# A transformer block's second norm, transposed by VectorE in 32x32 blocks instead of by TensorE

## The chip, the cores and the metric

One core of a Trainium2 chip runs the whole program. Its engines are TensorE (PE; its weight loads are listed apart as PEld), VectorE (DVE), ScalarE (ACT), GpSimd (POOL) and SyncE (SP), which mostly issues DMAs. The metric is the time on the device in microseconds (us) of one execution. The kernel before took 651.25 us, the median of three runs (650.94 to 652.86).

## The reference

Sixteen batches of 256 tokens with 256 features pass through one block in float32: a norm, attention with 16 heads of 16 features, a residual; a second norm, a gated feed-forward network with 1024 inner features, a residual. Cut to what matters:

```python
x = x + attn(layernorm(x), wq, wk, wv, wo)      # scores masked beyond 16 keys ahead, softmax
h = layernorm(x)                                # the second norm
gate = einsum('bsh,ih->bsi', h, gate_w)         # gate_w, up_w, down_w: Catmull-Rom
up   = einsum('bsh,ih->bsi', h, up_w)           # splines through control points
x = x + einsum('bsi,hi->bsh', silu(gate) * up, down_w)
```

The product of h with the gate and up weights sums over the features. On the chip that sum runs over partitions, so h, which the norm leaves with tokens on the partitions, has to be turned so that features lie there.

## The kernel before, in words

All of it is one software pipeline. The loop at the end of `block_kernel` runs 20 steps `s`; step `s` works on four batches at once: it projects queries, keys and values of batch `s+3`, takes row maxima of the scores of batch `nb = s-1`, exponentials and value products of batch `tb = s-2`, and the output projection, second norm and feed-forward network of `ob = s-3` and of the batch before it. Each engine runs its instructions in the order in which the source writes them: the class `InOrder` (line 78; its call on line 88 is the line that nearly every record of the profile carries) hands each to a call that keeps program order. So what stands ahead of what on an engine is read off the source, and the text of the loop is the schedule.

A step has numbered gaps. `inner` (twice two groups of heads) and `outer` (twice) make the scores on TensorE; between them `project(s, gap)` and `fill(s, gap)` put other TensorE work. `fill` holds a table: for `s < 13` the products `gate_up` 1, 2 and 3 of batch `s-4` stand in gaps 1, 3 and 4, `down` 0 (the first 128 tokens) in gap 5 and `down` 1 in gap 6. From `s = 13` on, where nothing is left to project, `down` is cut into halves over gaps 4, 5, 6 and 6.5. `gate_up` 0 of batch `s-3` stands in gap 7, at the step's end.

The scores go to two PSUM tiles of which there is one copy each; ScalarE reads them with an exponential, VectorE with `find_max` (a reduction of 144 or 256 columns to a maximum per row, eight of them after the last `outer`). Both have to be through before TensorE writes the next scores there.

The part that the change touches is the tail of a step: `project_o` (attention output added to x), `stats_f` (mean and variance on VectorE, the power -1/2 on POOL), `fill(s, 5)`, `norm_f` (two VectorE instructions that write the normed batch, tile `xnf`, tokens on the partitions), the last `outer`, `fill(s, 6)`, `turn_f`, `project(s, 6)` (values projection, tile `pv`), `fill(s, 6.5)`, `turn_max` (the maxima transposed, tile `pm`) and `fill(s, 7)`. `turn_f` calls `transposed` (line 244): four TensorE passes of 128x128 against an identity into a PSUM tile `ptf`, then one ScalarE copy into `x2T`, which all the gate and up products of the batch read (`pg`, `pu`).

The tiles of `down` (`pd`) and of the gate and up products share two PSUM buffers, tag "f"; `ptf`, `pv`, `pm` and the projections share two others, tag "m". VectorE adds each finished `pd` to x.

Of the kernel before, what the change touches and what calls it, by code (L numbers as in the profile page):

```python
# [11 lines left out]
F32 = mybir.dt.float32  # L12
# [6 lines left out]
P = 128  # L19
B, S, DIM = 16, 256, 256  # L20
# [73 lines left out]
def block_kernel(  # L94
# [14 lines left out]
    pe, dve, act, pool, sp = (  # L109
        InOrder(tc, e) for e in (nc.tensor, nc.vector, nc.scalar, nc.gpsimd, nc.sync)  # L110
    )

    const = ctx.enter_context(tc.tile_pool(name="const", bufs=1))
    sb = ctx.enter_context(tc.tile_pool(name="sb", bufs=2))
# [100 lines left out]
    xns, mxs, aus, aos, recs, x2s, x2Ts = ({} for _ in range(7))  # L215
# [28 lines left out]
    def transposed(src, dst, nm, engine=act):  # L244

        pt = ps_m.tile([P, 2, S], F32, tag="m", name=f"p{nm}")
        for kc in range(2):
            for c in range(2):
                pe.transpose(
                    pt[:, kc, c * P : (c + 1) * P],  # L250
                    src[:, c, kc * P : (kc + 1) * P],
                    ident,
                )
        copied(engine, dst, pt)
# [110 lines left out]
    def scores(qk, maxima, g, first, to, n):  # L365

        half = slice(first % P, first % P + HB)
        for r in range(4):
            q4 = slice(32 * r, 32 * r + HD + (0 if maxima else 1))
            on = 0 if maxima else 1  # L370
            pe.matmul(
                tiles[r // 2][half, r % 2, to : to + n],
                lhsT=qk[q4, on, g, first : first + HB],
                rhs=qk[q4, 1 - on, g, 0:n] if maxima else qk[q4, 0, g, S - n : S],
                start=True,
                stop=True,
            )

    def find_max(b, g, r, c, at, n):
        h = 4 * g + r  # L380
        seen = sb.tile([P, S], BF16, tag="seen", name=f"z{b}_{h}_{c}")
        dve.tensor_tensor_reduce(
            out=seen[:, 0:n],
            in0=tiles[r // 2][:, r % 2, at : at + n],
            in1=masks[c],
            scale=1.0,
            scalar=NEG,
            op0=ALU.add,
            op1=ALU.max,
            accum_out=mxs[b][:, c, h : h + 1],  # L390
        )

    def read(exponentials, maxima):

        for stage, pr in ((exponentials, 0), (maxima, 1), (exponentials, 1), (maxima, 0)):
            if stage:
                stage(pr)
# [31 lines left out]
    def outer(nb, tb, g2):  # L429
        has_n, has_t = 0 <= nb < B, 0 <= tb < B  # L430
        qn, qt = qks[nb % NQK], qks[tb % NQK]
        for gi in range(2):
            g, at = 2 * g2 + gi, W0 * gi
            if has_n:
                scores(qn, True, g, 0, at, HB + LOOK)
                scores(qn, True, g, HB, at, P + LOOK)
            if has_t:
                scores(qt, False, g, P, at + HB + LOOK, W1)
                scores(qt, False, g, P + HB, at + JB, W1 - HB)
        def exponentials(pr):  # L440
            e = sb4.tile([P, 2, 2, W1], F32, tag="e1", name=f"e1{tb}_{g2}_{pr}")
            act.activation(
                e,
                tiles[pr][:, :, 0 : 2 * W0].rearrange("p r (g c) -> p r g c", g=2)[
                    :, :, :, W0 - W1 : W0
                ],
                AF.Exp,
                scale=HD**-0.5,
            )
            pool.affine_select(  # L450
                out=e[:, :, :, 0:P], in_=e[:, :, :, 0:P],
                compare_op=ALU.is_ge, fill=0.0, base=I1 + LOOK - P,
                pattern=[[0, 2], [0, 2], [1, P]], channel_multiplier=-1,
            )
            es[tb, 1, g2, pr] = e

        def maxima(pr):
            for r in (2 * pr, 2 * pr + 1):
                for gi in range(2):
                    find_max(nb, 2 * g2 + gi, r, 0, W0 * gi, JB)  # L460

        read(exponentials if has_t else None, maxima if has_n else None)
# [86 lines left out]
    def norm_f(b):  # L549
        x2s[b] = normed(b, "f")  # L550

    def turn_f(b):
        x2Ts[b] = sb.tile([P, 2, S], F32, tag="x2T", name=f"x2T{b}")
        transposed(x2s.pop(b), x2Ts[b], f"tf{b}")

    def product(out, lhsT, rhs, start, stop, columns=P):
# [29 lines left out]
    def down(b, c, half=None, columns=P):  # L586

        inter = inters[b]
        if (b, c) == (B - 1, 1):

            for n in range(0, DIM, P):
                at = slice(n, n + P)
                pd = ps_f.tile([P, P], F32, tag="f", name=f"pd{b}_{c}_{n}")
                for ic in range(8):
                    pe.matmul(
                        pd, lhsT=inter[:, ic, P:], rhs=downT[:, ic, at],
                        start=(ic == 0), stop=(ic == 7),
                    )
                dve.tensor_tensor(xs[b][:, c, at], xs[b][:, c, at], pd, ALU.add)
                (act if n else sp).dma_start(out[b][P:, at], xs[b][:, c, at])  # L600
            return
        if half != 1:
            pds[b, c] = ps_f.tile([P, DIM], F32, tag="f", name=f"pd{b}_{c}")
        for ic in range(8) if half is None else range(4 * half, 4 * half + 4):
            product(
                pds[b, c], inter[:, ic, c * P : (c + 1) * P], downT[:, ic, :], ic == 0, ic == 7,
                columns,
            )
        if half == 0:
            return  # L610
        dve.tensor_tensor(xs[b][:, c, :], xs[b][:, c, :], pds.pop((b, c)), ALU.add)
        to = out[b].rearrange("(c p) d -> p c d", p=P)
        if b == B - 1:
            sp.dma_start(to[:, c, :], xs[b][:, c, :])
        elif c == 1:
            sp.dma_start(to, xs.pop(b))
# [37 lines left out]
    def do(stage, b, *args):  # L654
        if 0 <= b < B:
            stage(b, *args)
# [8 lines left out]
    def fill(s, gap):  # L665


        if s < B - AHEAD:
            order = (
                (1, gate_up, 1, 32), (3, gate_up, 2), (4, gate_up, 3, 32), (5, down, 0),  # L670
                (6, down, 1),
            )
        else:
            order = (
                (1, gate_up, 1, 32), (2, gate_up, 2), (3, gate_up, 3), (4, down, 0, 0, 32),
                (5, down, 0, 1), (6, down, 1, 0), (6.5, down, 1, 1),
            )
        for at, stage, *what in order:
            if at == gap:
                if s == B + 3 and stage is down:  # L680

                    if what[1] == 0:
                        down(B - 1, what[0])
                else:
                    do(stage, s - 4, *what)
        if gap == 7:
            do(gate_up, s - 3, 0)
# [3 lines left out]
    def part(i):  # L691
        spline(*parts[i])

    early = {
        (0, 1): ((stats_a, 1), (value_ones, 1)),
        (0, 2): (
            (norm_a, 1), (project_qk, 0), (spread, 0), (load_rest, 0), (coefficients, 0),
            (stats_a, 2), (scores_and_values, 2),
        ),
        (0, 4): ((turn_a, 1, dve), (project_v, 0, dve), (norm_a, 2), (part, 0)),  # L700
        (1, 1): ((turn_a, 2), (project_part, 1, 0), (stats_a, 3)),
        (1, 2): ((project_part, 1, 1), (spread, 1), (coefficients, 1)),
# [50 lines left out]
    for s in range(B + 4):  # L753
        nb, tb, ob = s - 1, s - 2, s - 3
        inner(nb, tb, 0)
        if ob < B - 1:
            do(values, ob, 1)
            do(gather, ob)
        project(s, 1)
        fill(s, 1)  # L760
        inner(nb, tb, 1)
        do(invert, ob)
        if s:
            do(load_x, s + 2 + AHEAD)
        project(s, 2)
        fill(s, 2)
        outer(nb, tb, 0)
        project(s, 3)
        fill(s, 3)
        inner(nb, tb, 2)  # L770
        do(values, tb, 0)
        project(s, 4)
        do(divide, ob)
        fill(s, 4)
        inner(nb, tb, 3)
        do(project_o, ob)
        do(stats_f, ob)
        project(s, 5)
        fill(s, 5)
        if s != 3:  # L780
            do(norm_f, ob)
        outer(nb, tb, 1)
        fill(s, 6)
        if s == 3:

            project(s, 6)
            norm_f(ob)
            turn_max(nb)
        do(turn_f, ob)
        if s != 3:  # L790
            project(s, 6)
        fill(s, 6.5)
        if tb == B - 1:
            values(tb, 1)
            gather(tb)
        if s != 3:
            do(turn_max, nb)
        project(s, 7)
        fill(s, 7)
# [30 lines left out]
```

## Time and profile before

| what | value |
|---|---|
| median of 3 runs | 651.25 us |
| the profiled execution's own time | 652.13 us |
| its span, first to last instruction | 650.4 us |
| mean granted TensorE clock in it | 0.997 |
| TensorE / VectorE / ScalarE / POOL busy | 642.7 / 369.2 / 216.4 / 129.5 us |
| ptf: 64 TensorE passes, mean of one | 275 ns |
| x2T: 16 ScalarE copies, mean of one | 585 ns |
| gate product to gate product, batches 5 to 6 | 38.09 us |
| gate product to gate product, batches 10 to 11 | 32.91 us |

The profile is one execution, recorded instruction by instruction. A group line gives the count of its instructions, their busy time in us, the mean of one in ns, and behind the second bar the idle time of the engine ahead of them with what ended it. A timeline line gives start and duration in us, and the idle time ahead in brackets. A name such as `x2T<-ptf` says which tile is written from which. TensorE's records overlap, since its matmuls are pipelined, so the distance from the start of one group to the start of the next is what it costs there, not the duration.

### The profile page before, as it was taken

Reading aid. Unit: us, or ns where it says so; the run is one execution under the profiler, and the core shown is the slowest. Engines: PE = TensorE matmul, PEld = TensorE weight load, DVE = VectorE, ACT = ScalarE, POOL = GpSimd, SP = SyncE. Lnnn points to the kernel's source line nnn. Section 1 sums busy time; section 2 is a strip of 40 time slices with the busy share of each in tenths; the row PEclk is TensorE's granted clock in tenths of the full one; section 3 lists DMA queues with packets and bytes.
Section 4 is the critical chain, followed back from the end, with each engine's and each line's share of the span. In section 5 each row is a group of like instructions: output and inputs, shape, how many; then the busy total and the mean of one; then the engine's idle time right before and its main releaser. Section 6 shows DMA issues by size and latency. Waiting matters only on the chain.

```text
span 650.4 us, 21144 instructions
## 1 busy us (share of the span) xinstructions
PE 642.7 (99%) x8740; PEld 477.3 (73%) x8740; DVE 369.2 (57%) x1483; ACT 216.4 (33%) x383; POOL 129.5 (20%) x254
## 2 busy tenths in 40 slices
PE   8999999999999999999999999999999999999998
PEld 7666667777778777787877778777777777777777
DVE  6785566646465664646566464655656565633342
ACT  1345543233332323333232332323333333333110
POOL 6232222111121211212112121211212030312000
PEclk9999899999999999999999999999999999999999
DMA  5843141414132131312213131210010101010100
GB/s 173 174 69 54 35 83 29 82 38 86 34 76 42 35 75 39 86 35 69 49 31 80 36 72 34 54 32 21 19 36 20 36 21 30 26 41 14 51 17 17
DMA packets 40768, 33.36 MB, mean 51 GB/s; under 512 B 10593, under 2 KB 40033, under 8 KB 40673
## 3 DMA queue, kind: packets, MB, share of 16 engines
q1 hardware_dynamic: 39392, 30.90, 21.7%
q8 instruction: 69, 1.13, 0.8%
q10 hardware_dynamic: 1280, 1.11, 0.6%
q14 instruction: 27, 0.21, 0.3%
HBM read 14.42 MB, written 4.47 MB: 29 GB/s over the span
## 4 chain that ended last, share of the span: by engine, by line
PE 96%; DMA 1%; DVE 1%; ACT 1%; issue 1%; POOL 0%; SPq 0%; ACTq 0%
PE pg L88 18%; PE pd L88 17%; PE pu L88 17%; PE scores L88 15%; PE po L88 7%; PE py L88 5%; PE pq L88 4%; PE pk L88 4%; PE pv L88 4%; PE pw L88 1%; PE ptf L88 1%; DMA qk<-qkc 1%; DMA x<-x 1%; PE pm L88 1%; PE pta L88 0%
## 5 line engine op out<-in xcount | busy, mean ns | idle before, releaser
L88 ACT ACTIVATE e<-scores 128x512 f32<-128x512 f32 (+1 forms) x192 | 117.5, 615 | 268.9 <-PE scores L88 222.6
L88 DVE CUSTOM_DVE_ANT_0 z<-scores,mask 128x144 bf16<-128x144 f32 (+1 forms) x512 | 154.7, 362 | 56.0 <-PE scores L88 33.3
L88 POOL TENSOR_SCALAR_AFFINE_SELECT e<-e 128x224 f32<-128x224 f32 (+1 forms) x192 | 93.8, 489 | 403.0 <-ACT e L88 402.6
L88 PE MATMUL pg<-x2T,gateT 128*32 128x256 f32 (+1 forms) x1112 | 124.0, 381 | 0.7 <-ACT x2T L88 0.7
L88 PE MATMUL pu<-x2T,upT 128*32 128x256 f32 (+1 forms) x1112 | 121.4, 379 | 0.0
L88 PE MATMUL pd<-downT,inter 128*128 128x256 f32 (+2 forms) x672 | 119.1, 376 | 0.0
L88 DVE SCALAR_TENSOR_TENSOR th<-th,pg 128x512 f32<-128x512 f32 x64 | 44.0, 688 | 113.4 <-ACT th L88 113.4
L88 PE MATMUL scores<-qk 17*64 17x144 f32 (+7 forms) x4096 | 106.5, 317 | 1.2 <-ACT e L88 1.1
L88 PEld LDWEIGHTS pd<-downT,inter 128*128 128x128 f32 (+1 forms) x672 | 93.3, 167 | 15.4 <-DVE th L88 0.3
L88 PEld LDWEIGHTS pu<-x2T,upT 128*32 128x32 f32 (+1 forms) x1112 | 85.3, 132 | 25.2
L88 PEld LDWEIGHTS pg<-x2T,gateT 128*32 128x32 f32 (+1 forms) x1112 | 81.8, 132 | 25.7 <-DVE inter L88 1.5
L88 PEld LDWEIGHTS scores<-qk 17*64 17x64 f32 (+1 forms) x4096 | 68.8, 131 | 39.1 <-issue 33.1
L88 ACT ACTIVATE th<-pg 128x512 f32<-128x512 f32 x64 | 38.2, 597 | 67.6 <-PE pg L88 67.0
L88 DVE TENSOR_TENSOR inter<-th,pu 128x512 f32<-128x512 f32 x64 | 44.0, 688 | 26.2 <-PE pu L88 26.2
L88 PE MATMUL po<-e,v 128*32 128x256 f32 (+1 forms) x1024 | 51.2, 342 | 0.0
L88 PEld LDWEIGHTS po<-e,v 128*32 128x32 f32 x1024 | 30.0, 111 | 24.3 <-issue 13.5
L88 DVE DVE_READ_ACCUMULATOR2_ANT mx<- 128x1 f32 x512 | 42.5, 83 | 0.1
L88 DVE TENSOR_TENSOR x<-x,pd 128x256 f32<-128x256 f32 (+1 forms) x33 | 13.6, 412 | 41.4 <-PE pd L88 41.4
L88 PE MATMUL pq<-xT,wq 128*128 128x256 f32 x128 | 31.7, 390 | 0.7 <-ACT xT L88 0.7
L88 PE MATMUL py<-wo,ac 128*128 128x256 f32 x128 | 31.9, 392 | 0.0
L88 PE MATMUL pv<-wv,xT 128*128 128x256 f32 x128 | 31.0, 385 | 0.4 <-ACT qkc L88 0.4
L88 PE MATMUL pk<-xT,wk 128*128 128x256 f32 x128 | 30.6, 381 | 0.0
(69 smaller groups left out, 384.0 us busy)
## 6 DMA issues: line engine op xcount, KB each, us to landing
qk<-qkc SPq DMA_DIRECT2D x124, 64.0 KB
x<-x SPq DMA_DIRECT2D x16, 256.0 KB
ac<-au SPq DMA_DIRECT2D x128, 32.0 KB
rb<-rd SPq DMA_DIRECT2D x32, 128.0 KB
out<-x SPq DMA_DIRECT2D x15, 256.0 KB
xT<-xT SPq DMA_DIRECT2D x9, 256.0 KB
fa<-ra SPq DMA_DIRECT2D x9, 128.0 KB
qk<-mxT SPq DMA_DIRECT2D x64, 4.0 KB
```

Of the source, the lines that this page charges most:

```text
L88: return self.tc.keep_in_program_order(fn(*args, **kwargs))
```

## The change

For batches 1 to 14, `turn_f` no longer calls `transposed`. VectorE's `transpose` turns blocks of 32x32. One instruction takes 32 tokens' partitions and 32 features of each of four (token half, feature half) pairs, 128 elements in each partition, and writes them to 32 feature partitions. Four groups `q` of source partitions by four groups `m` of destination partitions make sixteen instructions a batch. The four with `m = 0` are issued early, straight behind the norm; the other twelve in the place of the old `turn_f`. The order around them changes too: the norm and the early four come before `fill(s, 5)`, and for all batches but the last `turn_f` comes before `fill(s, 6)`. On VectorE this puts the residual adds of `down` 0 and `down` 1 behind the early four and behind the twelve. Batches 0 and 15 are turned as before.

```diff
-    def turn_f(b):
-        x2Ts[b] = sb.tile([P, 2, S], F32, tag="x2T", name=f"x2T{b}")
+    def turn_f(b, early=False):
+        if early or not 0 < b < B - 1:
+            x2Ts[b] = sb.tile([P, 2, S], F32, tag="x2T", name=f"x2T{b}")
+        if 0 < b < B - 1:
+            src = x2s[b].rearrange("p c (kc d) -> p c kc d", kc=2)
+            dst = x2Ts[b].rearrange("p kc (c t) -> p c kc t", c=2)
+            for m in (0,) if early else (32, 64, 96):
+                for q in range(0, P, 32):
+                    dve.transpose(
+                        dst[m : m + 32, :, :, q : q + 32], src[q : q + 32, :, :, m : m + 32]
+                    )
+            return
         transposed(x2s.pop(b), x2Ts[b], f"tf{b}")
...
         project(s, 5)
-        fill(s, 5)
         if s != 3:
             do(norm_f, ob)
+        if 0 < ob < B - 1:
+            turn_f(ob, True)
+        fill(s, 5)
         outer(nb, tb, 1)
-        fill(s, 6)
         if s == 3:
             project(s, 6)
             norm_f(ob)
             turn_max(nb)
-        do(turn_f, ob)
+        if ob < B - 1:
+            do(turn_f, ob)
+        fill(s, 6)
+        if ob == B - 1:
+            turn_f(ob)
         if s != 3:
             project(s, 6)
         fill(s, 6.5)
```

## The prediction

> **What bounds the kernel now.** I read the page first (busy times, clock, chain), then the groups by shape, then the timeline of each engine around the second norm's transpose, in a middle step and in a late one, and last the clock in short windows.
>
> ```profile
> PE 642.7 (99%) x8740; PEld 477.3 (73%) x8740; DVE 369.2 (57%) x1483; ACT 216.4 (33%) x383; POOL 129.5 (20%) x254
> PEclk9999899999999999999999999999999999999999
> PE 96%; DMA 1%; DVE 1%; ACT 1%; issue 1%; POOL 0%; SPq 0%; ACTq 0%
> ```
>
> TensorE is busy 99% of the span and is 96% of the chain that ended last, so whatever shortens its list of work gains, and whatever makes it stand still costs in full: no idle time is left to absorb it. VectorE's 57% is an average and does not say whether VectorE is free just where the new work falls. That takes the timeline. For the middle step in which batch 5 is normed:
>
> ```profile
> 277.87 0.69 POOL L88 TENSOR_TENSOR rstdf<-rstdf,neghalf 128x2 f32<-128x2 f32 x1 [2.04 <-DVE rstdf L88]
> 279.14 0.42 DVE L88 TENSOR_TENSOR x<-x,pd 128x256 f32<-128x256 f32 x1 [1.36 <-PE pd L88]
> 279.48 0.73 DVE L88 TENSOR_SCALAR xnf<-x,mvf,rstdf 128x256 f32<-128x256 f32 x2
> 280.44 0.31 DVE L88 CUSTOM_DVE_ANT_0 z<-scores,mask 128x144 bf16<-128x144 f32 x1 [0.23 <-PE scores L88]
> 282.27 0.08 DVE L88 DVE_READ_ACCUMULATOR2_ANT mx<- 128x1 f32 x1
> 283.67 0.60 PE L88 MATMUL ptf<-ident,xnf 128*128 128x128 f32 x4
> 284.10 1.89 PE L88 MATMUL pv<-wv,xT 128*128 128x256 f32 x8
> 284.30 0.59 ACT L88 COPY x2T<-ptf 128x512 f32<-128x512 f32 x1 [2.11 <-PE ptf L88]
> 285.83 0.38 PE L88 MATMUL pm<-ident,mx 128*16 128x128 f32 x2
> 286.05 1.89 PE L88 MATMUL pg<-x2T,gateT 128*128 128x256 f32 x8
> ```
>
> (Columns: start, duration, both us; in brackets the idle time ahead and what ended it.) TensorE's four passes take 283.67 to 284.10, 0.43 us of its time; ScalarE's copy ends at 284.89, and the reader of x2T, the first gate product, starts at 286.05: 1.16 us of slack. VectorE norms from 279.48 to 280.21 and then has eight row maxima of the scores until 282.35.
>
> **What goes.** 14 batches x 0.43 us of TensorE = 6.0 us, all of it on the bound. ScalarE's copy (0.585 us x 14) goes too and is worth nothing: ScalarE waits for TensorE before and after it. The freed PSUM buffer turn of "m" is worth nothing: no TensorE wait for one appears in the list of waits, and the next users find buffers read at least a microsecond earlier.
>
> **What comes, and where.** Sixteen VectorE instructions of 32 partitions x 128 elements per batch. Call the time from one to the next T. Four stand between the norm and the maxima, twelve behind the maxima, and the gate product waits for the last. So x2T now ends a chain on VectorE, and I time it against TensorE. Middle step: the power on POOL ends at 278.56; the norm, moved ahead of the residual add of `down` 0, starts 0.04 later (so in batch 10: 467.26 to 467.30) and ends at 279.33; 0.04 for the write to be seen (a dependent `bn_aggr` starts that long after `bn_stats`); 4T; the add, now behind them, 0.34 from start to start; the maxima, 1.91; 12T; 0.06 to TensorE (batch 0: copy ends 94.00, gate starts 94.05). That is 281.68 + 16T. Unhindered, TensorE would be there at 286.05 - 0.43 = 285.62. A stall begins at T = 0.246 and eats the gain at T = 0.273.
>
> **T.** No row of before transposes. Nearest rows:
>
> ```profile
> L88 DVE CUSTOM_DVE_ANT_0 z<-scores,mask 128x144 bf16<-128x144 f32 x256 | 61.2, 304 | 14.4 <-PE scores L88 9.9 <-ACT qkc L88 4.3 <-issue 0.3
> L88 DVE TENSOR_TENSOR x<-x,pd 128x128 f32<-128x128 f32 x2 | 0.6, 288 | 2.9 <-PE pd L88 2.9
> L88 PE MATMUL ptf<-ident,xnf 128*128 128x128 f32 x64 | 10.0, 275 | 0.0
> ```
>
> Low end 0.195 us: the two norm instructions start 0.33 apart with 256 elements though each lasts 0.41, and 128 elements less at 1.04 ns each (from the 421 and 304 ns of the maxima at 256 and 144 columns) take off 0.133. That needs neighbours to overlap as those do. High end 0.43: a full 0.30 plus a second 0.133, if a transposed element takes two cycles. I take 0.30, the whole duration of a 128 to 144-element instruction without overlap (288 and 304 ns), because each of the sixteen reads another group of 32 partitions than its neighbour, and every overlap in the trace is between instructions on the same partitions.
>
> The Trainium skill, "VectorE: DVE Perf Modes", section "Two Vector instructions with no wait between them", says that an instruction whose input or output starts in another 32-partition quadrant than the last one starts only when all earlier ones have finished; and its section on the three transpose paths gives 311 ns for a VectorE pass over 128x128 in bf16 and, in the rules for kernel authors, leaves a 128x128 transpose to TensorE. No run here shows it yet. By that figure, as an estimate, T is 0.31 and the sum below 2.2 us higher; by the overlap of the rows it would be 16 lower.
>
> **The sum at T = 0.30.** Batches 1 to 9 (period 38.09 us, all alike): ready 286.48, +0.43 each, x9 = +3.9. Batches 10 to 13 are where the cover is gone: no values projection is left, and half of `down` 1 stands on either side of the transpose.
>
> ```profile
> 466.57 0.69 POOL L88 TENSOR_TENSOR rstdf<-rstdf,neghalf 128x2 f32<-128x2 f32 x1 [1.95 <-DVE rstdf L88]
> 467.30 0.73 DVE L88 TENSOR_SCALAR xnf<-x,mvf,rstdf 128x256 f32<-128x256 f32 x2 [0.49 <-POOL rstdf L88]
> 468.92 0.60 PE L88 MATMUL ptf<-ident,xnf 128*128 128x128 f32 x4
> 471.30 1.89 PE L88 MATMUL pg<-x2T,gateT 128*128 128x256 f32 x8
> ```
>
> The norm ends only 3.27 us ahead of the gate (middle: 5.84). Ready: 468.03 + 0.04 + 0.34 + 1.91 + 0.06 + 16T = 470.38 + 4.8 = 475.18, +3.88 each, x4 = +15.5. Batch 14 has no maxima: norm 597.09 to 598.14, ready 598.58 + 4.8 = 603.38 against 602.03, +1.35. Together +20.8; each 0.01 us of T moves it by up to 2.2.
>
> The clock: TensorE stands still some 4.3 us in each of the four late steps. Before has no such gap (0.7 us at most after the start); it halves its clock once:
>
> ```profile
> 68.00:69.00 1.00, 1.00 (x32) 0.46 (x31) 0.79 (x2) 0.00 (x1) 0.00 (x0) 0.72 0.02 7
> 69.00:70.00 1.00, 1.00 (x16) 0.40 (x12) 0.59 (x3) 0.60 (x1) 0.00 (x0) 0.50 0.02 5
> 71.00:72.00 1.00, 1.00 (x17) 0.40 (x9) 0.90 (x5) 0.00 (x0) 0.35 (x1) 0.58 0.00 0
> ```
>
> The clock is the third number from the end: 0.50 for 3.4 us, 68.44 to 71.84 by the shares of the first and last window, after a stretch of sparse weight loads. It lost 1.7 us. So 0 to 4 x 1.7; I take two, +3.4. "TensorE: Matmul & The Clock Gate" (Part 1) of the Trainium skill puts the drop after one idle window of some 3.4 us that runs freely; a 4.3 us gap holds a whole one about one time in four, which would make it one halving, +1.7 (an estimate).
>
> The residual adds are later: `down` 0's frees its PSUM buffer at 280.9 where pg wants it at 286; `down` 1's, now behind twelve transposes, ends near 286.9 and pu wants that buffer 1.7 us after pg. VectorE's tanh product behind it waits for pg anyway. Nothing moves on POOL's queue; on SP's the store of the batch goes out some 3 us later, ahead of the next load into that buffer by a whole step (10 buffers): nothing. Sum: +20.8 + 3.4 = +24.2. The profiled execution took 652.13 (650.4 of span), 0.9 above the median of the runs, 651.25; I set the difference on the median: 675.
>
> **Rivals.**
> - *The transposes overlap* (T = 0.195). For: the norms and maxima do. Against: changing partitions. Middle steps: no stall, -0.43 x 9 = -3.9; late: 473.50, +2.20 x 4 = +8.8; batch 14 -0.3. +4.6: 656.
> - *Two cycles an element* (T = 0.43). For: no row shows that a transpose runs at the rate of a copy. Against: no row has two cycles for plain reads either. +22.6 + 23.8 + 3.4 = +50, and up to 6.8 for the clock: 701 to 708.
> - *Not slower: VectorE has room.* For: 57% busy, 1.16 us of slack in the middle steps. It takes T so short that the late steps don't undo the middle ones: at the bare 0.133 of 128 elements the sum is still +4.8 - 3.9 - 0.4 = +0.5, so the sign turns just under T = 0.13; with no stall at all 645. Against: a `tensor_scalar` on two columns alone lasts 168 ns.
> - *The work moves and nothing follows*, a sum within 2 us: T between 0.10 and 0.17.
>
> **How the numbers follow.** Stalls with T 0.25 to 0.36: 0.64 (+9.6 without halving to +34.2 + 6.8, so 661 to 692); overlap 0.16; two cycles 0.13; nothing follows 0.03; not slower 0.04. The likeliest gives 675. The range takes in the overlap and the upper bound of the first, with a little more for T up to 0.38, and leaves out 0.19: 655 to 697. Within 0.3%, 2 us, a measurement can't tell a change from none: faster 0.04, same 0.03, slower 0.93.
>
> **What would show it.** Right: sixteen transposes a batch with starts about 0.30 apart; TensorE waiting for x2T before pg, about 0.9 us in the middle steps and 4.3 in batches 10 to 13; period 38.5 and 36.8 where it was 38.09 and 32.91; short windows of clock 0.5 behind the long waits. Wrong: starts 0.2 apart, no wait in the middle steps, or a wait before pm or scores rather than pg. The term most likely to fail is T.

## The result

The changed kernel took 688.12 us (median of 6 runs, 685.57 to 689.35) where the kernel before, run beside it, took 652.03 (6 runs): a ratio of 1.0545, with a 95% interval of 1.0523 to 1.0567. It is 36 us slower. The forecast of 675 was on the right side and its range held the time; it was 13 us short. The profiled execution took 688.14 us with a span of 686.4, 36.0 more than the span before.

The page of the changed kernel (busy times, granted clock in tenths over 40 slices, the chain that ended last by engine and by line):

```profile
PE 648.1 (94%) x8684; PEld 477.0 (69%) x8684; DVE 436.7 (64%) x1707; ACT 208.3 (30%) x369; POOL 129.4 (19%) x254
PEclk9999999999999999999999999999998999989999
PE 72%; DVE 20%; DMA 2%; issue 2%; POOL 2%; SPq 1%; ACT 1%; DVEq 0%; ACTq 0%
PE pg L88 17%; PE pu L88 16%; PE scores L88 12%; DVE x2T L88 9%; PE po L88 7%; PE py L88 5%; PE pq L88 4%; PE pk L88 4%; PE pd L88 4%; DVE z L88 3%; DVE x L88 2%; PE pv L88 2%; DVE xnf L88 1%; DVE statsf L88 1%; POOL rstdf L88 1%
```

TensorE's share fell from 99% to 94%, and its busy time rose from 642.7 to 648.1 us though it has 56 passes fewer; a fifth of the chain now runs over VectorE, and the largest VectorE item is the tile x2T. The clock line has two slices of 8 near the end that the page before has not. The groups and TensorE's list of waits name the instruction and the price of one transpose (group: count, busy us, mean ns; waits: us in total, times, longest):

```profile
L88 DVE STREAM_TRANSPOSE x2T<-xnf 32x128 f32<-32x128 f32 x224 | 67.8, 303 | 3.6
```

```profile
PE pg L88 <- DVE x2T L88: 24.7, 14, 3.4
PE pm L88 <- DVE mx L88: 3.7, 4, 0.9
```

All 14 turned batches make TensorE wait at the first gate product, `pg`. The timeline of the middle step in which batch 5 is normed (start and duration in us):

```profile
282.57 1.24 DVE L88 STREAM_TRANSPOSE x2T<-xnf 32x128 f32<-32x128 f32 x4
283.84 0.42 DVE L88 TENSOR_TENSOR x<-x,pd 128x256 f32<-128x256 f32 x1
286.12 3.79 DVE L88 STREAM_TRANSPOSE x2T<-xnf 32x128 f32<-32x128 f32 x12
288.60 0.38 PE L88 MATMUL pm<-ident,mx 128*16 128x128 f32 x2
289.97 1.99 PE L88 MATMUL pg<-x2T,gateT 128*128 128x256 f32 x8 [0.99 <-DVE x2T L88]
291.80 1.89 PE L88 MATMUL pu<-x2T,upT 128*128 128x256 f32 x8
```

Twelve transposes in 3.79 us are 0.316 from start to start; the last ends at 289.91 and `pg` starts 0.06 later. From `pg` to `pu` it takes 1.83 us, where it took 1.73 before: after the wait the first weights are loaded in the open. The weight loads of the two profiles show it (PEld; the kernel before first):

```profile
285.94 1.60 PEld L88 LDWEIGHTS pg<-x2T,gateT 128*128 128x128 f32 x8
289.97 1.59 PEld L88 LDWEIGHTS pg<-x2T,gateT 128*128 128x128 f32 x8 [1.28 <-DVE x2T L88]
```

Before, the first load started 0.11 us ahead of the first pass at 286.05; now both start at 289.97. The period of a step is 38.90 us, +0.81. The late step of batch 10, and the clock in it (in the windows the third number from the end):

```profile
478.89 3.79 DVE L88 STREAM_TRANSPOSE x2T<-xnf 32x128 f32<-32x128 f32 x12
479.01 0.38 PE L88 MATMUL pm<-ident,mx 128*16 128x128 f32 x2 [0.93 <-DVE mx L88]
482.83 3.23 PE L88 MATMUL pg<-x2T,gateT 128*128 128x256 f32 x8 [3.45 <-DVE x2T L88]
485.86 2.36 PE L88 MATMUL pu<-x2T,upT 128*128 128x256 f32 x8
```

```profile
480.00:482.00 2.00, 0.00 (x0) 0.00 (x0) 1.92 (x7) 0.00 (x0) 0.00 (x0) 1.00 0.00 0
482.00:484.00 2.00, 1.17 (x4) 1.06 (x5) 1.08 (x4) 0.00 (x0) 0.00 (x0) 0.84 0.00 0
484.00:486.00 2.00, 2.00 (x6) 1.56 (x6) 0.00 (x0) 0.00 (x0) 0.00 (x0) 0.50 0.40 136
486.00:488.00 2.00, 2.00 (x9) 1.53 (x7) 0.69 (x1) 0.60 (x1) 0.00 (x0) 0.80 0.03 7
```

TensorE waits 0.93 us ahead of `pm` and 3.45 ahead of `pg`; then the clock is at 0.50 for 3.44 us (0.64 + 2 + 0.80), and eight records of `pg` take 3.03 us to the start of `pu` instead of 1.73.

The 36.0 us of span, read from gate product to gate product:

| stretch | before | after | difference |
|---|---|---|---|
| start to batch 0's gate product | 94.05 | 92.63 | -1.4 |
| to batch 1's | 39.65 | 41.72 | +2.1 |
| batch 1's to batch 9's | 304.69 | 311.22 | +6.5 |
| batch 9's to batch 14's | 163.64 | 191.80 | +28.2 |
| to the end | 48.37 | 49.03 | +0.7 |

In the first row the profile of before has its one window of half clock and the other has none. The second holds, beside batch 1's +0.8, a wait of 1.07 for the DMA of the maxima, which e8 below has too (0.78), with batch 1 turned by TensorE. The fourth is the bulk: in batches 10 to 13 four chains of 4.3 us and, as read below, 9.1 us of half clock, and batch 14's 1.9.

### The profile page after: what moved, and what is told of

Same layout as the page of the kernel before. It is cut to its first block, busy times and chain, and to the rows that moved or that the text cites. A ratio compares the mean times of both kernels' runs of the same rounds, so it can differ in the third digit from the quotient of the medians.

```text
span 686.4 us, 21249 instructions
## 1 busy us (share of the span) xinstructions
PE 648.1 (94%) x8684; PEld 477.0 (69%) x8684; DVE 436.7 (64%) x1707; ACT 208.3 (30%) x369; POOL 129.4 (19%) x254
## 4 chain that ended last, share of the span: by engine, by line
PE 72%; DVE 20%; DMA 2%; issue 2%; POOL 2%; SPq 1%; ACT 1%; DVEq 0%; ACTq 0%
PE pg L88 17%; PE pu L88 16%; PE scores L88 12%; DVE x2T L88 9%; PE po L88 7%; PE py L88 5%; PE pq L88 4%; PE pk L88 4%; PE pd L88 4%; DVE z L88 3%; DVE x L88 2%; PE pv L88 2%; DVE xnf L88 1%; DVE statsf L88 1%; POOL rstdf L88 1%
## 5 line engine op out<-in xcount | busy, mean ns | idle before, releaser
L88 PE MATMUL pg<-x2T,gateT 128*32 128x256 f32 (+1 forms) x1112 | 131.6, 389 | 25.3 <-DVE x2T L88 24.7
L88 PE MATMUL pu<-x2T,upT 128*32 128x256 f32 (+1 forms) x1112 | 124.1, 382 | 0.0
L88 PEld LDWEIGHTS pg<-x2T,gateT 128*32 128x32 f32 (+1 forms) x1112 | 85.7, 136 | 55.2 <-issue 18.1
L88 PEld LDWEIGHTS pu<-x2T,upT 128*32 128x32 f32 (+1 forms) x1112 | 87.7, 135 | 26.4
L88 DVE STREAM_TRANSPOSE x2T<-xnf 32x128 f32<-32x128 f32 x224 | 67.8, 303 | 3.6
```

The lines of the kernel that those rows point to most:

```text
L88: return self.tc.keep_in_program_order(fn(*args, **kwargs))
```

## The experiments

The theory was that of the prediction: x2T ends a chain on VectorE, the chain is too long, shortly in the middle steps and by far in the late ones, and each long wait brings half clock. Rivals: the loss is spread evenly over batches; the new order of norm and `down` is what costs; the half clock has another cause; transposes never overlap.

### e1 and e8: one part of the batches at a time

```diff
-        if 0 < b < B - 1:
+        if 1 <= b < 10:        # e8: 10 <= b < 14
...
+        if 1 <= ob < 10:       # the new order of the loop for these alone
```

> VectorE transposes batches 1 to 9 alone; batches 10 to 14 keep TensorE's passes and the old order. Theory: the middle steps cost +0.81 us each (period 38.90 against 38.09), the late ones all the rest: 652.0 + 9 x 0.81 = 659, no window of half clock late in the run. Rival: the loss of 36 us is spread evenly over the 14 batches, 2.6 each: 675.

> VectorE transposes batches 10 to 13 alone; all others as before the change. Theory: 4 x 4.33 us of chain and 9 us of half clock: 652.0 + 17.3 + 9 = 678, waits of 0.93 ahead of pm and 3.45 ahead of pg. Rival: evenly spread loss, 4 x 2.6: 662.

e1 took 659.47 us, a ratio of 1.0136 (1.0110 to 1.0162) to the kernel before; period 38.90 in all eight middle steps, 32.9 to 33.0 in the late ones, and no half clock after the first 22 us but for the run's last microseconds, where TensorE's work ends. e8 took 676.98, 1.0389 (1.0371 to 1.0407). TensorE's waits for x2T:

```profile
PE pg L88 <- DVE x2T L88: 8.9, 9, 1.0
```

```profile
PE pg L88 <- DVE x2T L88: 13.8, 4, 3.4
PE pm L88 <- DVE mx L88: 3.7, 4, 0.9
```

The first line is e1's, the two others e8's. Against the kernel before in the same rounds nine middle batches cost 9 us (7.3 of them by the period), four late ones 26. The even spread is out.

### e2: the late waits filled

```diff
+    def pass_time(n):
+        run = ps_m.tile([P, 2 * S], F32, tag="m", name="idle")
+        for _ in range(n):
+            pe.matmul(run[:, 0:P], lhsT=ident, rhs=ident, start=True, stop=True)
...
+        if 10 <= ob <= 13:
+            pass_time(14)
         project(s, 7)
         fill(s, 7)
```

> The changed kernel with 14 passes of 128x128 of the identity against itself (0.216 us each, 3.0 us in all) put on TensorE between pm and the first gate product of batches 10 to 13, where it waits 3.45 us; their result is not used. Theory: the clock fell to half because TensorE stood still, which cost 1.7 + 3.0 + 1.7 + 2.7 = 9.1 us; kept busy it stays at 1.00 and the time is 688.1 - 9 = 679, the wait for x2T itself unchanged. Rival: the half clock has another cause: 688 or more.

It took 680.19 us (679.63 to 680.73): more work on TensorE, 8 us less than the changed kernel, or 6 when each is set against the kernel before in its own rounds (a ratio of 1.0450, 1.0425 to 1.0474, where the changed kernel had 1.0545). The timeline and the clock of the step of batch 10 (each of the 14 passes shows as two records):

```profile
480.08 3.29 PE L88 MATMUL idle<-ident 128*128 128x128 f32 x28
483.59 1.99 PE L88 MATMUL pg<-x2T,gateT 128*128 128x256 f32 x8 [0.23 <-DVE x2T L88]
```

```profile
482.00:484.00 2.00, 1.77 (x15) 1.56 (x14) 1.91 (x6) 0.00 (x0) 0.00 (x0) 1.00 0.00 0
484.00:486.00 2.00, 2.00 (x11) 1.77 (x10) 0.00 (x0) 0.38 (x1) 0.00 (x0) 1.00 0.39 133
```

x2T comes no sooner, but the clock stays at 1.00 and the late period is 37.18 in each of the steps that e2 fills, +4.27 against before, where the changed kernel had 38.9 to 40.2. From batch 9's gate product to batch 14's it takes 182.6 us instead of 191.8: 9.2 us, against the 9.1 read from the windows. (In batch 14's step, not filled, e2 had a window of half clock of its own, which takes 1.7 us back.) Standing still was the cause, since nothing but the filling was changed.

### e3: the new order with TensorE's passes

```diff
-        if 0 < b < B - 1:
-            src = ...
-            ...
-            return
         transposed(x2s.pop(b), x2Ts[b], f"tf{b}")
...
-        if 0 < ob < B - 1:
-            turn_f(ob, True)
```

> The new order of the loop, but every batch turned by TensorE's four passes and ScalarE's copy. Theory: the order alone costs little: in the late steps the passes now wait about 0.95 us for the norm, in batch 14 about 1.7, 652.0 + 4 x 0.95 + 1.7 = 657. Rival: the reordering of down and the norm is what costs: near 688.

656.44 us, 1.0085 (1.0063 to 1.0107). The middle period is 38.04, so the order costs nothing there; in the late steps TensorE waits for the norm, which `down` 1 no longer covers:

```profile
467.13 0.78 PE L88 MATMUL ptf<-ident,xnf 128*128 128x128 f32 x4 [0.70 <-DVE xnf L88]
```

That is +0.84 a late step and +1.6 in batch 14. The order is a small loss by itself, not the 36.

### e4 and e5: what makes a transpose dear

```diff
-                        dst[m : m + 32, :, :, q : q + 32], src[q : q + 32, :, :, m : m + 32]
+                        dst[m : m + 32, :, :, q : q + 32], src[m : m + 32, :, :, q : q + 32]
```

> Sixteen transposes of the same size as in the changed kernel, each from 32 partitions to the same 32, four in a row on the same ones, so that the blocks are not exchanged between partition groups (this leaves the exchange out). Theory: neighbours on the same partitions overlap, 0.20 us from start to start in 12 of 16 places instead of 0.316, chain 1.4 us shorter: middle steps without a wait (-1.24 each against the changed kernel), late ones -1.4: 670, or down to 661 if the clock then holds. Rival: transposes never overlap: 0.316 and 688.

664.84 us, 1.0212 (1.0182 to 1.0242). The group and the twelve of a middle step:

```profile
L88 DVE STREAM_TRANSPOSE x2T<-xnf 32x128 f32<-32x128 f32 x224 | 49.5, 271 | 1.3
```

```profile
280.34 2.69 DVE L88 STREAM_TRANSPOSE x2T<-xnf 32x128 f32<-32x128 f32 x12
```

Twelve take 2.69 us instead of 3.79. The fourth, fifth and sixth of them, one by one:

```profile
280.96 0.26 DVE L88 STREAM_TRANSPOSE x2T<-xnf 32x128 f32<-32x128 f32 x1
281.23 0.30 DVE L88 STREAM_TRANSPOSE x2T<-xnf 32x128 f32<-32x128 f32 x1
281.46 0.26 DVE L88 STREAM_TRANSPOSE x2T<-xnf 32x128 f32<-32x128 f32 x1
```

The fifth is on other partitions than the fourth and starts 0.01 us after the fourth has ended; the sixth is on the fifth's partitions and starts 0.07 before the fifth has ended. Over the twelve, starts are 0.20 to 0.24 apart on the same partitions and 0.27 where the partitions change, though no instruction of e4 writes to another group than it reads. The middle steps have no wait and a period of 37.65, 0.44 us under the kernel before, which is what the change was to save. So it is the change of partitions from one transpose to the next that keeps them from overlapping. The Trainium skill says so ("VectorE: DVE Perf Modes", section "Two Vector instructions with no wait between them": an instruction that starts in another quadrant of partitions waits until the earlier ones have finished), and 0.316 against 0.20 agrees with it. The clock still fell in three of the four late steps, behind waits of 0.43 and 2.34 us.

```diff
-            for m in (0,) if early else (32, 64, 96):
-                for q in range(0, P, 32):
-                    dve.transpose(
-                        dst[m : m + 32, :, :, q : q + 32], src[q : q + 32, :, :, m : m + 32]
-                    )
+            if early:
+                dve.transpose(dst, src)
```

> One VectorE transpose of 128 partitions x 512 elements per batch behind the norm in place of the sixteen; 32x32 blocks are turned in their own partition group (this leaves the exchange between groups out). Theory: the sixteen cost 16 x 0.17 us of fixed time plus 128 elements each; four groups side by side take 512 x 1.04 ns + 0.17 = 0.70 us against 5.06. The chain is then 4.4 us shorter, the wait for x2T gone in the middle steps and 0.2 us in the late ones: 652.0 - 14 x 0.43 + 0.8 = 647. Rival: the 512 elements run one group after another, 2 us and more: 652 to 660.

647.74 us, 0.9939 (0.9920 to 0.9957). One line of its groups:

```profile
L88 DVE STREAM_TRANSPOSE x2T<-xnf 128x512 f32<-128x512 f32 x14 | 10.0, 712 | 0.5
```

The same 65,536 elements take 0.71 us in one instruction and 16 x 0.316 = 5.06 in sixteen. Turning blocks is cheap. The other 4.3 us are the price of sixteen instructions on 32 partitions each, which is how the kernel takes blocks from one group of 32 partitions to another, and e5 leaves that out. About 1.6 us of it come from the change of partitions between neighbours: from the first start to the start of what follows, the four and the twelve take 1.27 + 3.83 us in the changed kernel and 0.81 + 2.72 in e4, which also leaves the exchange out. The rest, 2.8, is that of sixteen instructions on a quarter of the partitions in place of one on all. Other ways across the groups were not tried.

### e6: an add taken off the chain

```diff
+        if c == 0 and 0 <= b < B - 2:
+            held.append(b)
+        else:
+            add(b, c)
...
             do(turn_f, ob)
+        while held:
+            add(held.pop(), 0)
         fill(s, 6)
```

> The changed kernel with the residual add of down 0 moved behind the twelve transposes. Theory: the add lies on the chain and its 0.34 us come off every wait for x2T: 688.1 - 14 x 0.34 = 683 (windows of half clock as before). Rival: the maxima behind it wait for the scores anyway, nothing comes off: 688.

689.26 us: nothing gained, and the reason was neither the theory's nor the rival's.

```profile
290.00 0.75 DVE L88 TENSOR_TENSOR x<-x,pd 128x256 f32<-128x256 f32 x2
290.47 1.99 PE L88 MATMUL pg<-x2T,gateT 128*128 128x256 f32 x8 [1.10 <-DVE x L88]
```

The transposes did finish earlier, but `pg` now waits for VectorE's write of x: the add reads the PSUM buffer of `pd` 0, and `pg` takes that buffer next. Behind the twelve transposes the add is again the last thing that `pg` needs, and the wait is 0.1 longer (1.10 for 0.99, period 39.01).

### e7: half by each engine, and only where there is cover

```diff
+    def turn_first(b):
+        pt = ps_m.tile([P, S], F32, tag="m", name=f"ptf{b}")
+        for c in range(2):
+            pe.transpose(pt[:, c * P : (c + 1) * P], x2s[b][:, c, 0:P], ident)
+        act.copy(x2Ts[b][:, 0, :], pt)
...
-        if 0 < b < B - 1:
+        if 1 <= b < 10:
...
-                        dst[m : m + 32, :, :, q : q + 32], src[q : q + 32, :, :, m : m + 32]
+                        dst[m : m + 32, :, 1, q : q + 32], src[q : q + 32, :, 1, m : m + 32]
...
+        if 1 <= ob < 10:       # the new order for these; turn_first(ob) behind fill(s, 6)
```

> Batches 1 to 9: feature half 0 by two TensorE passes and a copy of half the size behind down 1, feature half 1 by sixteen VectorE transposes of 64 elements; batches 10 to 14 as before the change. Theory: a transpose of 64 elements takes 0.25 us from start to start, the chain ends at 281.68 + 16 x 0.25 = 285.68 where TensorE arrives at 285.83 (times of the step of batch 5 before the change): no wait, two passes saved, 652.0 - 9 x 0.22 = 650. Rival: 64 elements take as long as 128 (0.316): wait of 0.9 us, 652.0 + 9 x 0.8 = 659.

649.85 us (12 runs) against 651.36: a ratio of 0.9967 (0.9955 to 0.9980), slightly faster than the kernel before.

```profile
L88 DVE STREAM_TRANSPOSE x2T<-xnf 32x64 f32<-32x64 f32 x144 | 34.0, 236 | 2.3
```

```profile
284.19 0.38 PE L88 MATMUL ptf<-ident,xnf 128*128 128x128 f32 x2
284.41 1.89 PE L88 MATMUL pv<-wv,xT 128*128 128x256 f32 x8
286.36 1.89 PE L88 MATMUL pg<-x2T,gateT 128*128 128x256 f32 x8
```

The transposes of 64 elements start 0.25 us apart, as expected. Two passes take 0.22 us from 284.19 to 284.41, `pg` has no wait, and the middle period is 37.87, 0.22 under that of before. Nine of these are the 2.0 us that were expected.

## Why the prediction was right in direction and 13 us short

- *TensorE is the bound, 0.43 us a batch are saved.* Right: without a wait (e4, e5) the middle period is 37.65 where it was 38.09.
- *x2T ends a chain on VectorE that TensorE waits for at pg.* Right, in all 14 batches. The sum 281.68 + 16T gives 286.74 with the measured T; the power on POOL ends 3.20 us later in the changed profile, which makes 289.94, and `pg` started at 289.97.
- *T = 0.30.* The mean duration was 303 ns, but the distance between starts is 0.316, with some 13 ns between neighbours. By the prediction's own rule (16 transposes in 14 batches) that is +3.6 us. The claim that they don't overlap, and the reason given, were borne out by e4.
- *A wait ends when x2T is there.* Missed: TensorE then loads the first weights in the open, 0.1 us in each of 14 batches, +1.4.
- *Batches 10 to 13 lose their cover, +3.88 each.* Right in kind: +4.27 with the clock held (e2), of which T and the first weights explain 0.36. Not foreseen was that 0.93 us of the wait would stand ahead of `pm`, since the maxima come later too; it adds nothing, because `pg` waits for the last transpose all the same. Batch 14: 1.35 forecast, 1.9 measured (from batch 13's gate product to batch 14's 33.88 us in e2, where this stretch has no half clock, against 32.01).
- *The clock, two halvings of 1.7 us.* This step failed: that only some of the late waits drop the clock, and that a drop lasts 3.4 us. All four late steps dropped, and in two of them the half clock lasted twice as long: 3.44, 6.84, 3.40 and 6.80 us in the windows of the profile. Less the part in which TensorE still waited, half of that is 1.7 + 3.0 + 1.7 + 2.7 = 9.1 us, +5.7 over the forecast and beyond the 6.8 that the range allowed for the clock (what goes with a drop, and with a second window, stands in the last section). The range held the time only because it also had room for a longer T.
- *The residual adds are later and it costs nothing.* Right for the changed kernel. How near `down` 0's add is to being the limit, e6 shows.

Together 24.2 + 3.6 + 1.4 + 5.7 = 34.9 of the 36.0 us; batch 14 and the tail of the run are the rest.

Of the rivals, overlapping transposes would have been right for the same instructions on unchanging partitions (e4); two cycles an element is out (512 elements in 0.71 us); VectorE did not have the room.

## What to carry to other kernels

Time the new chain against the instruction that needs its result, step by step and separately for the steps at the end of a pipeline, where the work that covered it has run out: four batches of 14 made three quarters of this loss. On an engine with many small instructions, look at what each one's neighbour touches, because a change of partition group turned 0.20 us into 0.316 here; and where the waiting engine's clock follows its work, add the half clock behind each wait of some microseconds to its price. A part of the same idea, cut to the slack that the trace shows (e7), was worth 0.3%.

## What was not expected of the hardware

- The half clock lasted 3.4 us or 6.8 us, never between (but for two drops that the end of the run cut short). It came behind all four late waits in the changed kernel, in e6 and in e8, and in e4 behind three of four, where TensorE stood still for 0.43 + 2.34 us with a pass of 0.2 us between. "TensorE: Matmul & The Clock Gate" of the Trainium skill, Part 1, puts the drop behind a whole idle window of some 3.4 us. The lengths agree with such a window; waits of under 2.8 us in all that still dropped the clock do not, so an estimate from a whole idle window was too low. The middle steps' waits of 0.99 us never dropped it.
- The traces show what goes with a drop: how much of one window TensorE stands still. In every run with more than one drop the drops begin whole multiples of 3.413 us apart, to within 0.02, so each run's windows can be laid over its trace. In the late steps of the changed kernel, e2, e4, e6 and e8, all 16 windows at full clock in which TensorE stood still for 2.09 us or more were followed by half clock, and none with 1.96 or less was. A window of half clock was followed by a second one where TensorE still waited 0.83 us or more of it (seven times), by none at 0.51 or less (nine times). Two late windows of e4, each with the one behind it (length, then TensorE's busy time; the clock is the third number from the end):

```profile
504.88:508.29 3.41, 1.22 (x6) 1.12 (x7) 2.44 (x11) 0.25 (x1) 0.00 (x0) 1.00 0.00 0
508.29:511.70 3.41, 3.41 (x10) 2.66 (x9) 0.69 (x1) 0.60 (x1) 0.00 (x0) 0.50 0.25 83
542.42:545.83 3.41, 1.45 (x7) 1.33 (x8) 2.21 (x10) 0.02 (x1) 0.00 (x0) 1.00 0.07 23
545.83:549.24 3.41, 3.41 (x51) 2.40 (x53) 1.41 (x3) 0.64 (x2) 0.00 (x0) 1.00 0.20 65
```

- A window of half clock in the first 90 us comes and goes between profiles of kernels that are alike there: at 68 us in the kernel before, e3, e4 and e6, at 18 us in e1, at both in e7, at 86 us in e2, not at all in the changed kernel, e5 and e8. Except in e2 (1.63 us), TensorE stood still for no more than 0.14 us of the window ahead of it, so standing still is not its cause, and no run shows what is. Each is worth 1.7 us, which is most of the noise from which a difference under 0.3% has to be told.
